# Shared-expert steps of an MoE layer moved between the slot-planning steps of its four token groups

## The chip, the cores and the metric

The kernel runs on one core of a Trainium2 chip. The metric is the device time of one launch in microseconds (us). The core has engines that each take their own instructions strictly in the order in which they were written to that engine's queue: PE (TensorE, matrix products and transposes), DVE (VectorE), ACT (ScalarE, activation functions and copies), POOL (GpSimd, here mostly the issuer of indirect DMAs), and SP (SyncE, which issues the ordinary DMAs). An engine that waits for a semaphore holds up everything behind it in its own queue.

## The reference

The input x has 2 x 1024 tokens of 256 features in fp32. Six residual steps follow one another; `ffn` is a mixture of experts with always-on shared experts, `ln` a layer norm without gain:

```python
x = x + 0.5 * L0_ffn(ln(x))     # 8 experts of width 176, top 2; shared width 352
x = x + L0_attn(ln(x))          # RWKV block: time mix, then channel mix
x = x + 0.5 * L0_ffn(ln(x))     # the same weights again
x = x + 0.5 * L1_ffn(ln(x))     # 32 experts of width 96, top 6; shared width 192
x = x + L1_attn(ln(x))          # linear attention
x = x + 0.5 * L1_ffn(ln(x))

def L0_ffn(x):
    scores = softmax(x @ gate_w); w, i = top_k(scores, 2)
    routed = sum over the chosen experts e of w_e * (silu(x @ w_gate[e]) * (x @ w_up[e])) @ w_down[e]
    shared = silu(x @ sw_gate) * (x @ sw_up) @ sw_down
    return routed + shared

def L0_attn(x):                  # only what the change touches
    h = layer_norm(x); hh = h shifted by one token
    k = (h * tm_mk + hh * (1 - tm_mk)) @ Wk.T   # the same with tm_mv, tm_mr, cm_mk, cm_mr
```

## The kernel before

All of x stays in on-chip memory as 16 tiles of 128 tokens (128 partitions by 256 features). Four tiles make a group, so there are four groups, g = 0 to 3.

One L0 mixture (`sparse_moe` with layer "L0", called once before and once after the RWKV block; the two are called the first and the second mixture here) goes through these steps:

- **prep(g)**: normalizes the group's four tiles, transposes them on PE (L156, tile `pt`), copies the transposes back on ACT (L441, tile `xTs`), multiplies them by the router weights (L453, tile `lg`), and routes: `route` (L174 to L207) takes the softmax and the top 2 on DVE, with the exponential on ACT (L182).
- **plan(g)**: works out a slot for each (token, expert) pair, so that pairs of one expert lie together in blocks of 128. It is a run of small matmuls on PE (L469, L491, L493, L502, L518; tiles `count`, `rank`, `far`) between short DVE operations, and it ends in the index tile `idx` (L557). Group g needs the counts of group g - 1.
- **scatter(g)**: POOL issues eight indirect DMAs (L566), one for each tile and choice, that write the normalized rows to their slots in DRAM (`xs`). After each three of them POOL executes five short `still` memsets (L330, L333).
- **owners()** (L590 to L620): works out which expert owns each block.
- **shared(t0, t1)**: a generator of steps. A step computes the hidden layer of one tile (`shared_hidden`: two gate products `pg` of 352 columns on PE at L659, silu on ACT at L649, a product on DVE at L650), turns that of the tile before (`turn`: three transposes `ph` at L675, copies at L682), and multiplies that of the tile before it by the down weights and adds it to x (`py` at L700, L707). Eight tiles take ten steps.
- **blocks()**: 39 blocks; each is fetched from `xs` by SP (L717, tile `xb`), transposed (L726, tile `px`), multiplied by its expert's weights (L748, then `turn`, then L765) and stored to `ys` (L774). A fetch waits until all 32 scatters have landed. At most five fetches are in flight.
- **combine(g)**: POOL gathers the results back (L785) and DVE adds them to x (L797). It runs beside the blocks.

The tool that records the program does not keep the order in which the Python code issues instructions: it schedules each engine's queue itself, starting from the written order. So instructions can move ahead of others within a stretch, and the order on each engine is fixed when the program is built. Loops that run beside the blocks (`combine`, the RWKV preparation) are placed by a small planner (`Clock`) with estimated block durations, and `behind_blocks()` ties an instruction to the place after the latest block's last instructions.

In the first mixture the written order is: the four groups (`begin`: prep, plan, scatter for each, then owners), `load_rwkv` (which loads the RWKV weights and vectors), the gate weights, the shared experts of the first eight tiles, and then the blocks. Inside `load_rwkv` five small DVE operations (L891) compute 1 - v of the five mixing vectors as each vector's DMA is issued. In the second mixture the order is the same without `load_rwkv`, written out by `slots_of`, and the shared experts stand ahead of the gate weights.

Of the kernel before, what the change touches and what calls it, by code (L numbers as in the profile page):

```python
# [8 lines left out]
F32 = mybir.dt.float32  # L9
I32 = mybir.dt.int32  # L10
AF = mybir.ActivationFunctionType
ALU = mybir.AluOpType
AX = mybir.AxisListType

P = 128
D = 256
DC = D // P
# [5 lines left out]
NB = NTOK // TB  # L23
# [16 lines left out]
def moe_blocks(m, tiles=NT):  # L40
    return (tiles * P * m["K"] + m["E"] * (P - 1)) // P
# [14 lines left out]
def macaron_kernel(ctx: ExitStack, tc: tile.TileContext, a: dict, out: bass.AP):  # L56
    nc = tc.nc
# [59 lines left out]
    def load_square(pool, name):  # L117
        rows, cols = a[name].shape
        w = pool.tile([P, rows // P, cols], F32, name=f"w_{name}")
        nc.sync.dma_start(out=w, in_=a[name].rearrange("(c p) o -> p c o", p=P))  # L120
        return w
# [165 lines left out]
    def fill_slots(xs, n, behind=None):  # L287

        zero = const.tile([P, D], F32, tag="zero", name=f"zero_{n}")
        nc.gpsimd.memset(zero, 0.0)  # L290
        d = nc.sync.dma_start(
            out=xs.rearrange("(n p) d -> p n d", p=P),
            in_=zero.unsqueeze(1).to_broadcast([P, n, D]),
        )
        if behind is not None:
            tc.add_manual_dep(d.ins, behind.name, SYNC, reason="not beside the blocks' loads")
# [10 lines left out]
    class Clock:  # L307
# [46 lines left out]
        def run(self, us):  # L354

            self.end = self.now + us
            while True:
                t = min(self.threads, default=None, key=lambda t: (t[0], t[1]))
                if t is None or t[0] > self.end:
                    break  # L360
                self.now = max(self.now, t[0])
                try:
                    t[0] = next(t[2])
                except StopIteration:
                    self.threads.remove(t)
            self.now = self.end
# [6 lines left out]
        def begin(self, rank, thread):  # L373
            self.threads.append([self.now, rank, thread])
# [13 lines left out]
    @contextmanager  # L388
    def behind_blocks():
        with ExitStack() as st:  # L390
            for d in clock.block.values():
                st.enter_context(tc.issue_after(d))
            yield

    HT = NT // 2
# [485 lines left out]
    rw = {}  # L881

    def load_rwkv(pool):
        for v in ("ln1_g", "ln1_b", "ln2_g", "ln2_b", "tm_first", "tm_mk", "tm_mv", "tm_mr", "cm_mk", "cm_mr"):
            t = pool.tile([P, DC], F32, name=f"v_{v}")
            with nc.allow_non_contiguous_dma(reason="256 numbers, once"):
                nc.sync.dma_start(out=t, in_=a[v].rearrange("(c p) -> p c", p=P))
            rw[v] = t
            if "_m" in v:
                u = pool.tile([P, DC], F32, name=f"u_{v}")  # L890
                nc.vector.tensor_scalar(u, t, -1.0, 1.0, ALU.mult, ALU.add)  # L891
                rw[f"1-{v}"] = u
        for m in ("WkT", "WvT", "WrT", "WoT", "WcrT", "WkeyT", "WvalT"):
            rw[m] = load_square(pool, m)

    def shifted(src, g, bias, tag, b, before, name):


        n = quad(rw["in"], "xn", f"n_{name}", bufs=1)
        normalize(src, n, BT, name)  # L900
        hT = rw["in" if tag == "h1T" else "pool"].tile(
            [P, DC, TB + 1], F32, tag=tag, name=f"hT_{name}", bufs=2
        )
        if before is None:
            nc.vector.memset(hT[:, :, 0:1], 0.0)
        else:
            nc.vector.tensor_copy(hT[:, :, 0:1], before[:, :, TB : TB + 1])
        for c in range(DC):
            nc.scalar.activation(
                hT[:, c, 1 : TB + 1],  # L910
                transposed(n, c, name),
                AF.Identity,
                bias=bias[:, c : c + 1],
                scale=g[:, c : c + 1],
            )
        return hT
# [146 lines left out]
    def wait(done):  # L1063
        while not done():
            yield clock.now + 1.0
# [156 lines left out]

    rwkv = [time_mix_job(0)]

    def slots_of(b):
        def slots():
            m0["prep"](b)
            m0["plan"](b)
            every_step(m0["scatter"](b))

        return slots

    for b in range(1, NB):
        rwkv += [time_mix_job(b), channel_mix_job(b - 1)]
    rwkv.append(channel_mix_job(NB - 1))
# [1 line left out]
    def all_of(part):  # L1237
        for us in part:
            clock.run(us)

    def every_step(part):
        clock.pool = 0.0
        for _ in part:
            clock.pool = 0.0

    def given_rows(m, groups, added, rank=0):

        for g in groups:
            yield from wait(lambda: g in m["ready"])
            yield clock.now + 3.0  # L1250
            yield from m["combine"](g, rank)
            added.add(g)

    def begin(m):

        for g in range(m["groups"]):
            m["prep"](g)
            m["plan"](g)
            every_step(m["scatter"](g))
        m["owners"]()  # L1260

    fill = []

    def settle(*done):

        while not all(d() for d in done):
            if fill:
                all_of(fill.pop(0))
            else:
                clock.run(1.0)  # L1270
# [9 lines left out]
    with ExitStack() as rwkv_stack:  # L1280
        weights = rwkv_stack.enter_context(tc.tile_pool(name="rwkvw", bufs=1))
        rw["in"] = rwkv_stack.enter_context(tc.tile_pool(name="rwkv_in", bufs=1))
        begun = 2
        with tc.tile_pool(name="moe_L0_0", bufs=1) as pool:
            m = sparse_moe("L0", w0, "L0_0", x, xs["L0"], ys["L0"], pool, bufs=1)
            begin(m)
            load_rwkv(weights)
            for h in range(2):
                m["weights"](h)
            every_step(m["shared"](0, HT))  # L1290
            added = set()

            def first_jobs():
                for b in range(begun):
                    yield from wait(lambda: b in added)
                    rwkv[b][0]()

            clock.begin(0, given_rows(m, range(NB), added))
            clock.begin(1, first_jobs())
            all_of(m["blocks"]())  # L1300
            all_of(m["shared"](HT, NT))
            settle(lambda: NB - 1 in added)
        for h in range(2):
            fill_slots(xs["AB"[h]], moe_blocks(MOE["L1"], HT), behind=m["latest"]["add"])
            fill_slots(
                ys["AB"[h]][SURE["L1"] * P :, :],
                moe_blocks(MOE["L1"], HT) - SURE["L1"],
                behind=m["latest"]["add"],
            )
        clock.forget()  # L1310
        rw["pool"] = rwkv_stack.enter_context(tc.tile_pool(name="rwkv", bufs=1))
        early_pool = l0_stack.enter_context(tc.tile_pool(name="early", bufs=1, side="right"))
        m0 = sparse_moe(
            "L0",
            w0,
            "L0_1",
            x,
            xs["L0"],
            ys["L0"],
            early_pool,  # L1320
            bufs=1,
        )
        run(rwkv, begun)
# [4 lines left out]
    load_sparse(w1, "L1", None, 4)  # L1328

    m0["home"]["pool"] = moe_pool  # L1330
    for b in range(NB):
        slots_of(b)()
    m0["owners"]()
    every_step(m0["shared"](0, HT))
    for h in range(2):
        m0["weights"](h)

# [181 lines left out]
```

## Time and profile before

| what | value |
| --- | --- |
| median of 13 runs | 1514.8 us (1507.91 to 1520.51) |
| profiled execution | 1513.09 us, span of its instructions 1511.3 us |
| PE busy | 1277.0 us, 84% of the span |
| DVE, ACT, POOL busy | 740.9, 626.9, 665.5 us |
| the first mixture's groups, to its last scatter | about 8 to 91 us |
| the second mixture's groups, to its last scatter | about 463 to 534 us |

The span is counted from the first profiled instruction; times below are microseconds from there. A busy share is an average over stages that have different limits, so the two stretches in which the groups are planned must be read by themselves: there PE is busy only part of the time. The profile also gives the share of its full clock that TensorE was granted ("PEclk"); at 0.50 every matmul takes about twice as long.

### The profile page before, as it was taken

The page shows a single profiled execution, that of the slowest core. Times are in us where ns is not written, and L with a number is a line of the kernel's source. Part 1 is how long each engine was busy: PE and PEld are TensorE (multiplying, and loading weights), DVE is VectorE, ACT ScalarE, POOL GpSimd, SP SyncE. Part 2 cuts the span into 40 slices and gives each one's busy share as a digit, 9 for nine tenths or more (in the row PEclk, how much of TensorE's full clock was granted, in tenths as well). Part 3 has the DMA queues.
Part 4 walks back from the last instruction along what each step waited for, and adds up shares of the span by engine and source line. Part 5 has one row for each costly group of instructions (what it writes and reads, how often), then busy time and mean ns, then how long its engine had stood idle before and what let it go on. Part 6 is the DMA issues. An engine that isn't in the chain of part 4 may idle for free. (4 is left out here: it accounts for less than half of the span.)

```text
span 1511.3 us, 23078 instructions
## 1 busy us (share of the span) xinstructions
PE 1277.0 (84%) x6100; PEld 978.6 (65%) x6100; DVE 740.9 (49%) x2507; ACT 626.9 (41%) x1672; POOL 665.5 (44%) x1336
## 2 busy tenths in 40 slices
PE   6699889799998799899799789887859888649961
PEld 4677666365576677677588677675647676448941
DVE  5333446845534423564364367655527643416544
ACT  4033544586654133524345354442234443125510
POOL 1630522011102712477774455057765005676565
PEclk9589889799999599999899899988969988769985
DMA  9623424950008324335767575332254323348843
GB/s 284 219 75 109 129 73 157 312 192 1 0 0 191 99 87 130 113 108 149 242 198 242 171 211 157 115 106 98 84 151 149 121 76 129 107 149 265 254 144 94
DMA packets 195170, 214.94 MB, mean 142 GB/s; under 512 B 40892, under 2 KB 178012, under 8 KB 195036
## 3 DMA queue, kind: packets, MB, share of 16 engines
q1 hardware_dynamic: 170460, 146.22, 31.2%
q0 software_dynamic: 24576, 67.14, 14.4%
q8 instruction: 59, 0.97, 0.3%
q14 instruction: 75, 0.61, 0.1%
HBM read 103.04 MB, written 110.23 MB: 141 GB/s over the span
## 5 line engine op out<-in xcount | busy, mean ns | idle before, releaser
L785 POOL DMA_INDIRECT yk_L<-ys_L,idx_L x64 | 62.1, 970 | 187.0 <-DMA ys_L<-yb_L 124.0
L333 POOL MEMSET still<- 128x96 f32 x620 | 111.1, 179 | 35.6
L748 PE MATMUL pg_L_b<-L0gu,xbT_L 128*128 x312 | 110.6, 478 | 0.0
L566 POOL DMA_INDIRECT xs_L<-xn_L,idx_L x64 | 62.0, 969 | 74.6 <-DVE idx_L L557 36.7
L659 PE MATMUL pg_L<-L0sgu,xTs_L 128*128 128x352 f32 x256 | 90.7, 489 | 3.9 <-DVE h_L L650 3.9
L566 POOL DMA_INDIRECT xs_B<-axl_at,idx_L_1B x48 | 46.9, 977 | 100.9 <-DVE idx_L_1B L557 89.2
L785 POOL DMA_INDIRECT yk_L_0B<-ys_B,idx_L_0B x48 | 46.8, 975 | 83.0 <-DMA xb_L_0B<-xs_B 47.3
L765 PE MATMUL py_L_b<-L0down,hT_L_b 88*128 x312 | 81.5, 383 | 0.0
L785 POOL DMA_INDIRECT yk_L_0A<-ys_A,idx_L_0A x48 | 46.6, 971 | 64.4 <-DVE x L797 27.2
L650 DVE TENSOR_TENSOR h_L_b<-g_L_b,pg_L_b 128x176 f32<-128x176 f32 x78 | 26.2, 336 | 95.0 <-ACT g_L_b L649 72.8
L765 PEld LDWEIGHTS py_L_b<-L0down,hT_L_b 88*128 88x128 f32 x312 | 59.4, 194 | 19.7 <-issue 1.5
L748 PEld LDWEIGHTS pg_L_b<-L0gu,xbT_L 128*128 128x128 f32 x312 | 55.8, 197 | 19.4 <-issue 2.0
L934 PE MATMUL pkk_cm<-mk_cm,w_WkeyT 128*128 128x512 f32 x128 | 62.7, 622 | 5.3 <-DVE mk_cm L926 3.6
L659 PEld LDWEIGHTS pg_L<-L0sgu,xTs_L 128*128 128x128 f32 x256 | 48.7, 202 | 27.1 <-DVE h_L L650 5.6
L748 PE MATMUL pg_L_1A_b<-L1gu,xbT_L_1A 128*128 x272 | 63.4, 361 | 0.4 <-PE ph_L_1A_b L675 0.4
L785 POOL DMA_INDIRECT yk_L_1A<-ys_A,idx_L_1A x48 | 46.8, 976 | 29.3 <-DVE h_L_1B_b L650 11.6
L748 PE MATMUL pg_L_0B_b<-L1gu,xbT_L_0B 128*128 x272 | 59.4, 343 | 0.3 <-issue 0.2
L748 PE MATMUL pg_L_0A_b<-L1gu,xbT_L_0A 128*128 x272 | 58.8, 341 | 0.5 <-issue 0.4
L946 PE MATMUL pkv_cm<-w_WvalT,sk_cm 128*128 128x256 f32 x256 | 58.0, 379 | 0.1
L748 PE MATMUL pg_L_1B_b<-L1gu,xbT_L_1B 128*128 x272 | 57.4, 335 | 0.1
L649 ACT ACTIVATE g_L_b<-pg_L_b 128x176 f32<-128x176 f32 x78 | 24.8, 318 | 77.1 <-PE pg_L_b L748 70.5
L566 POOL DMA_INDIRECT xs_A<-xn_L_0A,idx_L_0A x48 | 46.8, 974 | 21.6 <-issue 12.4
(639 smaller groups left out, 3405.7 us busy)
## 6 DMA issues: line engine op xcount, KB each, us to landing
xs_A<-zero SPq DMA_DIRECT2D x1, 10112.0 KB
xs_B<-zero SPq DMA_DIRECT2D x1, 10112.0 KB
xb_L<-xs_L SPq DMA_DIRECT2D x78, 128.0 KB
ys_L<-yb_L SPq DMA_DIRECT2D x78, 128.0 KB
xb_L_0A<-xs_A SPq DMA_DIRECT2D x68, 128.0 KB
ys_A<-yb_L_0A SPq DMA_DIRECT2D x68, 128.0 KB
xb_L_0B<-xs_B SPq DMA_DIRECT2D x68, 128.0 KB
ys_B<-yb_L_0B SPq DMA_DIRECT2D x68, 128.0 KB
```

The source lines that it names most:

```text
L333: d = nc.gpsimd.memset(still, 0.0)
L566: d = nc.gpsimd.indirect_dma_start(out=xs, out_offset=bass.IndirectOffsetOnAxis(ap=idx[:, t, k : k + 1], axis=0), in_=sent[g][t - BT * g], ...
L649: nc.scalar.activation(g, pg[:, 0:width], AF.Silu)
L650: nc.vector.tensor_tensor(dst, g, pg[:, width : 2 * width], ALU.mult)
L659: nc.tensor.matmul(pg, xbT[:, c, i * P : (i + 1) * P], w["sgu"][:, c, u, :, :].rearrange("p z w -> p (z w)"), start=(c == 0), stop=(c == D ...
L748: nc.tensor.matmul(pg, xbT[:, c, :], w["gu"][:, c, bass.ds(e, 1), :, :].rearrange("p e z h -> p (e z h)"), start=(c == 0), stop=(c == DC - 1),
L765: mm = nc.tensor.matmul(py, hT[0:HP, k, :], w["down"][:, bass.ds(e, 1), k, :].rearrange("p e d -> p (e d)"), start=(k == 0), stop=(k == C ...
L785: d = nc.gpsimd.indirect_dma_start(out=yk, out_offset=None, in_=ys[0 : n * P, :], in_offset=bass.IndirectOffsetOnAxis(ap=idx[:, t, k : k + ...
L934: nc.tensor.matmul(ps, w[:, c, oc * P : (oc + 1) * P], src[:, c, :], start=(c == 0), stop=(c == DC - 1),)
L946: nc.tensor.matmul(ps, src[:, c, i * P : (i + 1) * P], w[:, c, :], start=(c == 0), stop=(c == n - 1),)
```

## The change

Three edits. First, `begin` now starts the generator of the first eight tiles' shared experts and takes three of its steps after each group's scatter; what is left (here nothing: 10 steps, taken as 3, 3, 3 and 1) is taken after `owners`. Second, both mixtures use `begin`, so `slots_of` and the separate calls of `shared(0, HT)` go. Third, `load_rwkv` only reserves the five 1 - v tiles; a new function `opposites` computes them, called by the planner's thread `first_jobs` behind the blocks, once group 0 of the first mixture has been added back and just before the first RWKV preparation.

```diff
             rw[v] = t
             if "_m" in v:
-                u = pool.tile([P, DC], F32, name=f"u_{v}")
-                nc.vector.tensor_scalar(u, t, -1.0, 1.0, ALU.mult, ALU.add)
-                rw[f"1-{v}"] = u
+                rw[f"1-{v}"] = pool.tile([P, DC], F32, name=f"u_{v}")
...
+    def opposites():
+
+        for v in [v for v in rw if v.startswith("1-")]:
+            nc.vector.tensor_scalar(rw[v], rw[v[2:]], -1.0, 1.0, ALU.mult, ALU.add)
...
-    def slots_of(b):
-        def slots():
-            m0["prep"](b)
-            m0["plan"](b)
-            every_step(m0["scatter"](b))
-
-        return slots
...
     def begin(m):
 
+        shared = m["shared"](0, HT)
         for g in range(m["groups"]):
             m["prep"](g)
             m["plan"](g)
             every_step(m["scatter"](g))
+            for _ in range(3):
+                next(shared, None)
         m["owners"]()
+        every_step(shared)
...
-            every_step(m["shared"](0, HT))
             added = set()
 
             def first_jobs():
                 for b in range(begun):
                     yield from wait(lambda: b in added)
+                    if b == 0:
+                        with behind_blocks():
+                            opposites()
                     rwkv[b][0]()
...
     m0["home"]["pool"] = moe_pool
-    for b in range(NB):
-        slots_of(b)()
-    m0["owners"]()
-    every_step(m0["shared"](0, HT))
+    begin(m0)
     for h in range(2):
         m0["weights"](h)
```

## The prediction

> **What bounds the kernel now.** I read the page first: the change lies in the two stretches where an L0 mixture plans its groups, so the averages say little there, but two rows do.
>
> ```profile
> PE 1277.0 (84%) x6100; PEld 978.6 (65%) x6100; DVE 740.9 (49%) x2507; ACT 626.9 (41%) x1672; POOL 665.5 (44%) x1336
> ...
> PEclk9589889799999599999899899988969988769985
> ...
> L566 POOL DMA_INDIRECT xs_L<-xn_L,idx_L x64 | 62.0, 969 | 74.6 <-DVE idx_L L557 36.7
> ```
>
> Read in the second row: the clock falls to half in the second of the 40 slices (the first mixture's groups) and again in the fourteenth (the second's). In the third: POOL waits for the indices of the scatters. So next I read the timeline of the second mixture's groups, engine by engine: PE, then DVE, then POOL, then SP and PE again.
>
> ```profile
> 486.49 0.34 PE L469 MATMUL count_L<-ones,taken_L 128*8 128x1 f32 x8 [2.99 <-DVE taken_L L202]
> ...
> 493.72 3.16 PE L453 MATMUL lg_L<-L0router,xTs_L 128*128 128x8 f32 x14 [0.45 <-ACT xTs_L L441]
> ...
> 499.86 0.34 PE L469 MATMUL count_L<-ones,taken_L 128*8 128x1 f32 x8 [2.99 <-DVE taken_L L202]
> ...
> 493.86 0.17 DVE L557 TENSOR_SCALAR idx_L<-top_L 128x8 int32<-128x8 f32 x1
> ...
> 507.24 0.17 DVE L557 TENSOR_SCALAR idx_L<-top_L 128x8 int32<-128x8 f32 x1
> ...
> 521.52 0.17 DVE L557 TENSOR_SCALAR idx_L<-top_L 128x8 int32<-128x8 f32 x1
> ...
> 494.31 0.96 POOL L566 DMA_INDIRECT xs_L<-xn_L,idx_L  x1 [0.46 <-issue]
> ...
> 507.69 0.96 POOL L566 DMA_INDIRECT xs_L<-xn_L,idx_L  x1 [0.53 <-DVE idx_L L557]
> ...
> 521.97 0.97 POOL L566 DMA_INDIRECT xs_L<-xn_L,idx_L  x1 [0.94 <-DVE same_L L629]
> ...
> 535.79 18.25 SPq L717 DMA_DIRECT2D xb_L<-xs_L  x12
> ...
> 543.02 0.38 PE L726 MATMUL px_L<-ident,xb_L 128*128 128x128 f32 x2
> ```
>
> To be seen: the groups' indices come 13.4 and 14.3 us apart, and each group's first scatter starts 0.3 us behind its index, POOL having waited under 1 us. The chain of a group (transposes, logits, routing, plan) is exactly as long as eight scatters: it has no slack. Within it PE idles some 3 us a group, while DVE routes. The fetches are issued at 535.79, but PE takes the first block only at 543.02, because it is still at the shared experts.
>
> The clock, from the windows view:
>
> ```profile
> 478.00:485.00 7.00, 5.16 (x45) 4.52 (x44) 2.35 (x17) 2.90 (x5) 2.81 (x3) 0.97 1.26 256
> 485.00:525.50 40.50, 31.23 (x160) 27.12 (x161) 18.73 (x136) 4.18 (x9) 30.59 (x66) 0.50 0.44 133
> 525.50:545.00 19.50, 19.50 (x93) 15.10 (x93) 5.62 (x16) 7.32 (x25) 6.62 (x15) 1.00 0.25 81
> ```
>
> Half clock through the plans (last but two column) although PE is busy for 31 of 40 us. In windows of one microsecond it is lost between 484 and 485 (0.79), after PE went idle at 483.5, and full again between 525 and 526 (0.73), 3.5 us after the shared gate products begin at 521.88.
>
> In the first mixture the same chain has one wait more, in DVE's timeline:
>
> ```profile
> 51.66 0.20 DVE L891 TENSOR_SCALAR u_tm_mk<-v_tm_mk 128x2 f32<-128x2 f32 x1 [5.13 <-DMA v_tm_mk<-in_tm_mk]
> ...
> 54.04 0.17 DVE L891 TENSOR_SCALAR u_cm_mr<-v_cm_mr 128x2 f32<-128x2 f32 x1 [0.64 <-DMA v_cm_mr<-in_cm_mr]
> 54.12 0.19 DVE L178 TENSOR_REDUCE mx_L<-lg_L 128x4 f32<-128x32 f32 x1
> ...
> 64.90 0.96 POOL L566 DMA_INDIRECT xs_L<-xn_L,idx_L  x1 [6.66 <-DVE idx_L L557]
> ```
>
> Group 2's logits are done at 47.96 (their matmuls run 44.80 to 47.96); its routing stands behind five operations that wait for DMAs, and starts at 54.12.
>
> **The change, part by part.** The built order of the changed program shows where the scheduler puts the shared steps on PE; POOL's and SP's orders stay as they were, but for one swap each far away. Prices, from the second mixture's rows at full and half clock: a gate product `pg` (one of two per tile) 1.18 (526.59 to 527.77) and 2.50 (521.88 to 524.38); a down product `py` 1.30 (528.10 to 529.40) and 2.57 (first mixture, two thirds from 81.59 to 83.30); the three transposes `ph` 0.33 (525.83 to 526.15) and 0.83 (519.68 to 520.51).
>
> *Group 1* (its index is now 13.3 us after group 0's). Ahead of its logits PE gets `ph` of tiles 0 and 1 (0.66), `py` 0 (1.30) and the first halves of the products of tiles 4 and 5 (2.36): +4.3. Their second halves fall into the 3 us in which DVE routes: free. In the plan, `py` 1 and `ph` 2: +1.6. PE comes there busy, so I take full clock: the plan's 5.5 us (486.49 to 492.0) include 1.04 of transposes that move behind, and the other 4.4 become about 2.4 (group 0's plan at full clock, two `far` products fewer, 478.15 to 480.0): -3.0. Sum +2.9.
>
> *Group 2.* Ahead of its logits: four gate products (4.72), `py` 2 and 3 (2.60), `ph` 3 and 4 (0.66): +8.0, at the full clock that such work had at 525.5. Transposes to logits then take about 3.5 instead of 4.95 (491.93 to 496.88): -1.4. Routing leaves PE idle, as now, and the clock was lost there between 484 and 485, so the plan is at half: -1.04 of transposes, + `py` 4 and `ph` 5 (3.4): +2.4. Sum +9.0.
>
> *Group 3.* Ahead of its logits `py` 5 and 6, `ph` 6 and 7: 3.3 at full, 6.8 at half clock; transposes to logits -1.4 or +1.0; `py` 7 in its plan +2.57. Between +4.5 and +10.4; I take 4.5, since the row of 521.88 gave the clock back within 3.5 us of such work.
>
> The sum is +16.4 on the last index, and as the chain has no slack, on the last scatter.
>
> *The other end.* PE is then free when the first block lands. In the later mixture whose first transposes do wait for it, fetch to start is 2.4 us (1340.7 to 1343.1), so blocks can begin at 538.2 and, in the first mixture (fetch 93.00), at 95.4. The first `py` of a block now stands at 552.44 and 110.86: 14.2 and 15.5 after. [...] I take 9.5: -4.7 and -6.0.
>
> *The differences.* Group 2's routing of the first mixture no longer waits: 54.12 - 48.0 = -6.1. The five operations (0.17 to 0.33) now stand on DVE among the adds of group 0, ahead of the RWKV statistics; their DMAs have long landed; DVE is under half busy there: 0, at most +1.1.
>
> *Small ones.* ACT loads tables twice more per mixture (1.28 each, once for group 2's exponential, once for the blocks' silu). The first lies beside 2.2 us of logits, the second beside the first block's product: 0; without cover +5.1 in all. DVE's extra products (0.34) and adds (0.42) end while PE works on: 0, bounds 0 and +3. The RWKV stage is reordered a little (two table loads more): 0, between -3 and +3.
>
> Sum: second mixture 16.4 - 4.7 = +11.7; first 16.4 - 6.1 - 6.0 = +4.3; together +16. Behind the mixtures PE is busy 95 of 100 us (500 to 700), so the delay is carried to the end. Against the profiled 1513.1 us (1.7 below the median of 1514.8) that gives 1529.
>
> [...] The row: from 488 to 491.5 PE never stops and the clock stays at half. [...]
>
> **Rivals.** *The clock stays full* through routing and plans because PE has work between. Then the groups add 2.9, 8.0 - 1.4 + 1.6 - 3.1 = 5.1, and 3.3 - 1.4 + 1.3 - 2.1 = 1.1, together 9.1; blocks gain 7.2 and 8.5: second mixture +1.9, first -5.5. 1509.5, faster by 0.24%. For it: the half clock is dear now. Against it: groups 2 and 3 still have nothing on PE while DVE routes, and 3 us of that cost the clock after 484. It decides once the clock is full in both groups' plans. *The clock stays low*: group 2's burst starts at half (+1.7) and group 3 costs 10.4: 24 per mixture, less 3.9 and 5.2 at the blocks and the 6.1: +33, 1546. For it: light plans never lifted the clock in 40 us. Against: gate products did in 3.5. *No difference*: the shared steps cost the chain only what PE's idle time now holds (9 us a mixture), 16.4 - 9 = 7.4 a mixture, less 4.7, 6.0 and 6.1: -2, 1511 to 1514. Against it: the built order puts only group 1's second halves there.
>
> **How the numbers follow.** Within 0.2% (3 us) a change of this kernel can't be told from none. Chances: the forecast 0.72 (1520 to 1537), low clock 0.13, full clock 0.10, no difference 0.05. The range of 8 in 10 runs from 1514 to 1540; it leaves out most of the full clock and the upper half of the low one. Slower 0.85, same 0.06, faster 0.09.
>
> **What would show it.** Index tiles of the second mixture about 16, 22 and 19 us apart; POOL waiting 3 to 9 us before groups 1 to 3; the last scatter some 15 us later in its stage; PE idle for about 15 us before the first `px`, which starts within 3 us of the first fetch; no L891 wait. Wrong if POOL's waits stay under 1 us, or if the clock is 1.00 through the plans.

## The result and the profile after

The changed kernel takes 1535.7 us (median of 10 executions, 1528.5 to 1540.5) where the kernel before takes 1515.0 (46 executions): a ratio of 1.0128, 95% interval 1.0111 to 1.0145, some 19 us slower. The profiled execution took 1526.9 us (span 1525.1), 13.8 more than the one profiled before. It lies 8.8 us below its own median; that is taken up below.

First the page of the changed kernel, the rows that answer to those shown before:

```profile
PE 1271.6 (83%) x6100; PEld 970.4 (64%) x6100; DVE 738.6 (48%) x2507; ACT 632.6 (41%) x1678; POOL 663.4 (43%) x1336
...
PEclk9859999799999869899899889997879997769985
...
L566 POOL DMA_INDIRECT xs_L<-xn_L,idx_L x64 | 61.8, 966 | 101.3 <-DVE h_L L650 28.7
```

PE is busy for 5 us less, and of the two slices at half clock in the groups (the second and the fourteenth before; the last of the 40 is at half in both kernels) one is left, the third: by averages the kernel got no worse. The third row tells the other side: POOL's idle time ahead of the scatters went from 74.6 to 101.3 us.

The second mixture in DVE's timeline (the four index tiles), then in POOL's (the first scatter of groups 1, 2 and 3), then in SP's and PE's (the first fetch, the first transpose, the first down product of a block). Columns as before: start, duration, engine, line, operation, and in brackets the idle time before it with what ended it.

```profile
484.30 0.17 DVE L557 TENSOR_SCALAR idx_L<-top_L 128x8 int32<-128x8 f32 x1
...
500.45 0.17 DVE L557 TENSOR_SCALAR idx_L<-top_L 128x8 int32<-128x8 f32 x1
...
522.22 0.17 DVE L557 TENSOR_SCALAR idx_L<-top_L 128x8 int32<-128x8 f32 x1
...
540.27 0.17 DVE L557 TENSOR_SCALAR idx_L<-top_L 128x8 int32<-128x8 f32 x1
...
500.90 0.96 POOL L566 DMA_INDIRECT xs_L<-xn_L,idx_L  x1 [3.32 <-DVE same_L L629]
...
522.67 0.96 POOL L566 DMA_INDIRECT xs_L<-xn_L,idx_L  x1 [8.97 <-DVE idx_L L557]
...
540.72 0.96 POOL L566 DMA_INDIRECT xs_L<-xn_L,idx_L  x1 [4.75 <-DVE same_L L629]
...
554.49 12.28 SPq L717 DMA_DIRECT2D xb_L<-xs_L  x12
...
556.62 1.19 PE L726 MATMUL px_L<-ident,xb_L 128*128 128x128 f32 x4 [15.79 <-DMA xb_L<-xs_L]
...
565.18 1.03 PE L765 MATMUL py_L_b<-L0down,hT_L_b 88*128 x4
```

The indices come 16.2, 21.8 and 18.1 us apart (13.4 and 14.3 before). POOL, whose eight scatters last 12 to 13 us, now waits 3.32, 8.97 and 4.75 us before groups 1 to 3. PE then idles 15.8 us for the first block, and needs 10.7 us from fetch to the first down product where it needed 16.7.

The first mixture, in POOL's and DVE's timelines:

```profile
47.22 0.96 POOL L566 DMA_INDIRECT xs_L<-xn_L,idx_L  x1 [4.08 <-DVE same_L L629]
...
69.70 0.96 POOL L566 DMA_INDIRECT xs_L<-xn_L,idx_L  x1 [9.68 <-DVE idx_L L557]
...
90.10 0.96 POOL L566 DMA_INDIRECT xs_L<-xn_L,idx_L  x1 [7.09 <-DVE same_L L629]
...
56.41 0.19 DVE L178 TENSOR_REDUCE mx_L<-lg_L 128x4 f32<-128x32 f32 x1 [4.04 <-PE lg_L L453]
```

The routing of group 2 (last row) no longer stands behind the vectors, but behind its own logits on PE, and starts at 56.41, later than the 54.12 of before.

To compare kernels I use two stage times, read from each profile: from the start of a mixture's first scatter to the start of the first L765 product of its blocks. They leave out most of what the change does not touch.

| kernel | first mixture | second mixture | ratio to before, 95% interval |
| --- | --- | --- | --- |
| before | 78.98 | 70.86 | 1 |
| changed | 85.44 | 79.85 | 1.0128 (1.0111 to 1.0145) |
| e1 differences only | 71.99 | 70.79 | 0.9933 (0.9916 to 0.9950) |
| e2 steps only | 85.40 | 79.94 | 1.0168 (1.0145 to 1.0191) |
| e3 changed, routing filled | 80.08 | 79.72 | 1.0113 (1.0091 to 1.0134) |
| e4 a step in each routing | 70.72 | 67.86 | 0.9993 (0.9972 to 1.0014) |
| e5 second mixture only | 71.94 | 89.22 | 1.0073 (1.0046 to 1.0100) |
| e6 first mixture only | 84.74 | 71.82 | 1.0075 (1.0050 to 1.0100) |
| e7 a step in three routings | 67.81 | 67.25 | 0.9909 (0.9879 to 0.9939) |
| e8 e4's second, first as before | 71.93 | 65.91 | 0.9922 (0.9898 to 0.9946) |
| e9 e1 again | 72.34 | 70.88 | 0.9962 (0.9948 to 0.9975) |
| e10 changed again | 86.42 | 79.82 | 1.0134 (1.0105 to 1.0164) |
| e11 e7's first, e4's second | 68.17 | 69.76 | 0.9925 (0.9908 to 0.9941) |
| e12 changed, plans fed | 79.81 | 77.97 | 1.0119 (1.0095 to 1.0142) |

e1 to e4 ran on one chip, e5 to e8 on a second, e9 to e12 on a third. The kernel before took 1518.2 us on the first and the third and 1495.6 on the second, so only ratios are compared between chips. In the profiles that difference lies behind the second mixture's first block product: 940 to 947 us to the end of the span on the second chip (e5: 1504.2 - 562.90 = 941), 959 to 969 on the others.

The changed kernel's stages took 6.46 and 8.99 us more than before, 15.45 together; the RWKV stretch between them 1.84 less (370.72 to 368.88), the start before the first scatter 0.87 less, the rest behind 1.06 more: 13.80.

### The profile page after: what moved, and what is told of

Same layout as the page of the kernel before. It is cut to its first block, busy times and chain, and to the rows that moved or that the text cites. A ratio compares the mean times of both kernels' runs of the same rounds, so it can differ in the third digit from the quotient of the medians.

```text
span 1525.1 us, 23069 instructions
## 1 busy us (share of the span) xinstructions
PE 1271.6 (83%) x6100; PEld 970.4 (64%) x6100; DVE 738.6 (48%) x2507; ACT 632.6 (41%) x1678; POOL 663.4 (43%) x1336
## 3 DMA queue, kind: packets, MB, share of 16 engines
q0 software_dynamic: 24576, 67.14, 14.3%
## 5 line engine op out<-in xcount | busy, mean ns | idle before, releaser
L748 PE MATMUL pg_L_b<-L0gu,xbT_L 128*128 x312 | 113.7, 490 | 0.4 <-ACT xbT_L L730 0.4
L566 POOL DMA_INDIRECT xs_L<-xn_L,idx_L x64 | 61.8, 966 | 101.3 <-DVE h_L L650 28.7
L659 PE MATMUL pg_L<-L0sgu,xTs_L 128*128 128x352 f32 x256 | 87.1, 471 | 3.7 <-DVE h_L L650 3.7
L765 PE MATMUL py_L_b<-L0down,hT_L_b 88*128 x312 | 81.9, 385 | 0.0
L765 PEld LDWEIGHTS py_L_b<-L0down,hT_L_b 88*128 88x128 f32 x312 | 59.5, 194 | 19.9 <-issue 1.2
L726 PE MATMUL px_L<-ident,xb_L 128*128 128x128 f32 x156 | 31.3, 287 | 39.7 <-DMA xb_L<-xs_L 31.4
```

The source lines that it names most:

```text
L566: d = nc.gpsimd.indirect_dma_start(out=xs, out_offset=bass.IndirectOffsetOnAxis(ap=idx[:, t, k : k + 1], axis=0), in_=sent[g][t - BT * g], ...
L659: nc.tensor.matmul(pg, xbT[:, c, i * P : (i + 1) * P], w["sgu"][:, c, u, :, :].rearrange("p z w -> p (z w)"), start=(c == 0), stop=(c == D ...
L726: nc.tensor.transpose(px[:, c * P : (c + 1) * P], xb[:, c * P : (c + 1) * P], ident)
L748: nc.tensor.matmul(pg, xbT[:, c, :], w["gu"][:, c, bass.ds(e, 1), :, :].rearrange("p e z h -> p (e z h)"), start=(c == 0), stop=(c == DC - 1),
L765: mm = nc.tensor.matmul(py, hT[0:HP, k, :], w["down"][:, bass.ds(e, 1), k, :].rearrange("p e d -> p (e d)"), start=(k == 0), stop=(k == C ...
```

## Experiments: the parts one by one

**e1: the differences alone.** The kernel before with one part of the change:

```diff
-                u = pool.tile([P, DC], F32, name=f"u_{v}")
-                nc.vector.tensor_scalar(u, t, -1.0, 1.0, ALU.mult, ALU.add)
-                rw[f"1-{v}"] = u
+                rw[f"1-{v}"] = pool.tile([P, DC], F32, name=f"u_{v}")
...
+                    if b == 0:
+                        with behind_blocks():
+                            opposites()
                     rwkv[b][0]()
```

> The kernel before with one edit of the change: the five 1 - v operations are computed by opposites() behind the blocks; the shared steps stay where they were. Theory A (the prediction's term of -6.1): group 2's routing in the first mixture no longer waits for the vectors, POOL's wait of 6.66 us ahead of group 2's first scatter goes (under 1 us is left), everything behind it is 6 us earlier: 1509 us, -0.4%. Rival B (the wait is passed on): another late DMA or DVE's order holds group 2 as long; 1515 us, and POOL still waits over 4 us there.

1507.9 us, ratio 0.9933. e1's DVE and POOL in the first mixture's group 2:

```profile
47.51 0.19 DVE L178 TENSOR_REDUCE mx_L<-lg_L 128x4 f32<-128x32 f32 x1 [1.46 <-PE lg_L L453]
...
58.30 0.96 POOL L566 DMA_INDIRECT xs_L<-xn_L,idx_L  x1 [0.55 <-issue]
```

The routing starts with its logits, POOL's wait of 6.66 is 0.55, the stage is 7.0 us shorter. Theory A: this part of the change is a gain. How large is less sure than one run says: e9, the same kernel on a third chip, was expected at 0.9933 within 0.002 and with executions within 4 us, and came out at 0.9962 with executions 7 us apart. By these two runs the gain is 0.4 to 0.7%, and the ratios of one kernel from two chips lie 0.3% apart.

**e2: the shared steps alone**, the same hunks undone in the changed kernel.

```diff
-                rw[f"1-{v}"] = pool.tile([P, DC], F32, name=f"u_{v}")
+                u = pool.tile([P, DC], F32, name=f"u_{v}")
+                nc.vector.tensor_scalar(u, t, -1.0, 1.0, ALU.mult, ALU.add)
+                rw[f"1-{v}"] = u
...
-                    if b == 0:
-                        with behind_blocks():
-                            opposites()
```

> The changed kernel with the differences put back into load_rwkv; the shared steps stand between the groups in both mixtures. Theory A, as the prediction added it up: the wait for the vectors (6.1 us) comes back on top of the shared steps: 1542 us, 6 above the changed kernel's 1535.7. Rival B: the two do not add. The shared steps alone make group 2's logits of the first mixture late (56.3 us in the changed kernel's profile, against 54.0 when the last of the five was done before), so the wait lies beside PE's work: 1536 us, equal to the changed kernel within 2 us, and the five operations are done before group 2's routing could start.

1541.4 us, theory A's number. But the wait is in another place than theory A had it. e2's DVE, in the slot computation of group 1:

```profile
47.31 0.19 DVE L546 SCALAR_TENSOR_TENSOR slot_L<-rank_L,slot_L 128x32 f32<-128x32 f32 x1
...
50.34 0.17 DVE L891 TENSOR_SCALAR u_tm_mk<-v_tm_mk 128x2 f32<-128x2 f32 x1 [2.84 <-DMA v_tm_mk<-in_tm_mk]
...
52.42 0.17 DVE L891 TENSOR_SCALAR u_cm_mr<-v_cm_mr 128x2 f32<-128x2 f32 x1 [0.61 <-DMA v_cm_mr<-in_cm_mr]
...
53.13 0.17 DVE L557 TENSOR_SCALAR idx_L<-top_L 128x8 int32<-128x8 f32 x1
```

In the order that was built here the five operations stand in the middle of group 1's slots and hold its index until 53.13 (46.78 in the changed kernel): POOL waits 10.08 us before group 1 instead of 4.08. In the profile groups 2 and 3 make most of that good again (7.50 and 4.75 instead of 9.68 and 7.09), and the stage is 85.40 for the changed kernel's 85.44: there the two delays do not add, as theory B said, though not by its account, since it is a different group that waits. The medians are 0.4% apart (the intervals just touch), but the profiles put that elsewhere: of the 8 us by which e2's span is longer, 5.8 lie behind the second mixture's first block product (965.7 and 959.9). That theory A's number came out is therefore not shown to be the wait for the vectors.

**e5 and e6: one mixture each**, the differences moved in both. The diff of e5 (e6 has 3 and 0 exchanged):

```diff
-    def begin(m):
+    def begin(m, n):
...
-            for _ in range(3):
+            for _ in range(n):
                 next(shared, None)
...
-            begin(m)
+            begin(m, 0)
...
-    begin(m0)
+    begin(m0, 3)
```

> The changed kernel with the first mixture written as before (its eight shared tiles behind the groups); the second mixture and the differences as changed. Theory A (each mixture pays for its own groups, the differences pay back once): the differences alone took 1507.9 us; first scatter to first product of a block takes 79.9 us in the second mixture of the changed kernel's profile and 70.8 where only the differences moved: +9.1, 1517 us. Theory B (the 9 us by which the changed kernel's median lies above its profiled execution come from the second mixture): 1526 us, with executions more than 8 us apart.

> The reverse: the shared steps between the groups of the first mixture alone, the second mixture as before, the differences moved. Theory A: first scatter to first product of a block 85.4 us in the changed kernel's profile, 72.0 with only the differences moved: +13.4, 1521 us; together with the run of the second mixture alone the two delays add up to the changed kernel's. Theory B (the changed kernel's spread between executions, 12 us, comes from the first mixture, whose steps stand beside loads that fill the DMA engines): 1526 to 1530 us, with executions more than 8 us apart, and those of the second mixture alone within 4.

1.0073 and 1.0075. Against e1's 0.9933 each mixture costs 1.4% (1.1% against e9's 0.9962), more than the 0.6 and 0.9% that theory A took from the profile; the two add up to 2.8% (2.2%), and the changed kernel lies 2.0% above e1 on other chips, 1.7% on one chip (e10's median 1538.3 and e9's 1512.1). On the spread, e5's executions lie 15 us apart, as its theory B asked, and e6's 7, where its theory B asked for over 8 and for e5's within 4: neither mixture is shown to be the only source. e5's own profile shows why its second mixture is dearer than the changed kernel's, with the same instructions in the same order. First POOL, then the windows view of e5 (window; length; busy time and count of PE, PEld, DVE, ACT, POOL; granted clock; DMA share; GB/s):

```profile
492.84 0.95 POOL L566 DMA_INDIRECT xs_L<-xn_L,idx_L  x1 [6.91 <-DVE same_L L629]
...
518.27 0.96 POOL L566 DMA_INDIRECT xs_L<-xn_L,idx_L  x1 [12.61 <-DVE idx_L L557]
...
538.59 0.97 POOL L566 DMA_INDIRECT xs_L<-xn_L,idx_L  x1 [7.00 <-DVE same_L L629]
...
482.00:485.00 3.00, 2.48 (x20) 1.60 (x18) 2.59 (x23) 2.14 (x5) 1.93 (x8) 1.00 1.15 305
485.00:488.00 3.00, 3.00 (x15) 2.58 (x15) 0.27 (x2) 0.00 (x0) 0.94 (x1) 0.72 0.37 127
488.00:491.00 3.00, 3.00 (x12) 2.38 (x11) 1.41 (x7) 0.53 (x2) 0.00 (x0) 0.50 0.00 0
...
497.00:500.00 3.00, 3.00 (x15) 2.22 (x14) 1.03 (x4) 0.85 (x3) 2.30 (x8) 1.00 0.25 90
```

and the same stretch, group 1's plan, of the changed kernel:

```profile
493.00:496.00 3.00, 2.48 (x24) 1.88 (x22) 2.01 (x17) 1.15 (x5) 2.24 (x7) 1.00 1.16 309
496.00:499.00 3.00, 3.00 (x17) 2.48 (x18) 1.33 (x6) 0.53 (x2) 1.27 (x2) 1.00 0.83 220
499.00:502.00 3.00, 3.00 (x15) 2.28 (x14) 2.57 (x19) 0.85 (x3) 1.10 (x2) 1.00 0.00 0
```

In the one execution group 1's plan runs at full clock, in the other the clock falls to half in it and stays there for some ten microseconds of plan and shared work, with PE busy for 3.00 of 3.00. The groups wait 26.5 us instead of 17.0. The last section has the two executions side by side.

## Experiments: the clock

**e3: PE fed through the routing.** Unused gate products between logits and plan of groups 2 and 3 of the changed kernel:

```diff
+        def again(t):
+
+            _, xbT, i = places(t)
+            W = SH // SU
+            pz = bank("py", f"pz_{name}_{t}")[:, 0 : 2 * W]
+            for z in range(4):
+                nc.tensor.matmul(
+                    pz,
+                    xbT[:, 1, i * P : (i + 1) * P],
+                    w["sgu"][:, 1, z % 2, :, :].rearrange("p z w -> p (z w)"),
+                    start=(z == 0),
+                    stop=(z == 3),
+                )
...
             m["prep"](g)
+            if g > 1:
+                m["again"](BT * g)
             m["plan"](g)
```

> The changed kernel, and PE gets four gate products more (352 columns each, their result is not used) between the logits and the plan of groups 2 and 3, in both mixtures, so that it is not idle for the 3 us of the routing. The computation is otherwise the changed kernel's. Theory A (the groups' cost is partly the half clock that the idle routing brings): PEclk 1.00 in the plans of groups 2 and 3; by the changed kernel's rows that takes about 3 and 6.5 us off group 2's plan (second and first mixture) and 4.5 off each of group 3's: 18 us in all, 1517 us (1512 to 1524). Rival B (the delay is the number of products ahead of the logits, and the clock's fall lies beside waits for DVE and POOL): no change within 4 us, 1532 to 1540, whatever the clock does.

1534.7 us, 1.0113: theory B's number, and a miss of 18 us for A. The products stand where they should (507.0 to 509.6 in the second mixture, the plan's first matmul 0.57 us behind them), but the clock does not stay. e3's windows over group 2's plan:

```profile
510.00:512.00 2.00, 1.80 (x21) 1.76 (x21) 1.09 (x7) 0.00 (x0) 0.81 (x1) 1.00 0.22 74
512.00:514.00 2.00, 2.00 (x10) 1.65 (x9) 0.20 (x1) 0.00 (x0) 0.00 (x0) 0.81 0.02 4
514.00:516.00 2.00, 2.00 (x9) 1.65 (x8) 0.99 (x4) 0.53 (x2) 0.00 (x0) 0.50 0.00 0
```

It falls at 513.2, inside the plan (0.81 over 2 us), with PE busy for 2.00 of 2.00; in the changed kernel it fell at 512.5, 2.5 us into 3.04 us of idle time. So here it fell without the idle time of the routing. The first mixture took 5.4 us less in this one profile, the second no less.

**e12: the plans fed as well**, two more such products inside each group's plan:

```diff
+            if name[0:2] == "L0":
+                again(lo, 2)
             pb = bank("pt", f"far_{sub}")
...
+            if g > 1:
+                m["again"](BT * g, 4)
```

> The changed kernel with unused gate products that keep PE at wide work: four of 352 columns between logits and plan of groups 2 and 3 as in the run that filled the routing, and two more inside every group's plan, ahead of far. They add 1.2 us of PE to each group's chain (some 10 us in all with group 0's). Theory A (in the plans the clock falls although PE is busy, because products of 1 to 32 columns do not keep it up; that is where the spread and half of the groups' cost come from): PEclk 1.00 through all plans, executions within 6 us of each other, ratio 1.000 to 1.007, so faster than the changed kernel in spite of more work. Theory B (the clock is not what delays the groups): the added work shows, ratio 1.013 to 1.025, spread 12 us as before.

1.0119, executions 1530 to 1541. e12's windows over the plans of groups 1, 2 and 3 of the second mixture:

```profile
494.00:497.00 3.00, 2.48 (x22) 1.84 (x21) 1.90 (x16) 1.00 (x5) 2.24 (x7) 1.00 1.10 293
...
515.00:518.00 3.00, 3.00 (x20) 2.21 (x16) 0.75 (x5) 0.00 (x0) 0.10 (x1) 1.00 0.13 46
...
530.00:533.00 3.00, 2.58 (x22) 2.36 (x23) 1.29 (x8) 0.00 (x0) 2.42 (x5) 0.92 0.27 93
533.00:536.00 3.00, 3.00 (x17) 1.75 (x16) 0.00 (x0) 0.00 (x0) 1.88 (x7) 0.50 0.24 87
```

With wide products in it, the clock stays full through the plans of groups 1 and 2 and falls only in group 3's (0.92 of the third window). The stages are 6.6 and 1.9 us shorter than in e10 on the same chip, although 1.2 us of PE were added to the chain of each of groups 1 to 3: by that the half clock costs an estimated 10 us in the first mixture and 5.5 in the second (6.6 and 1.9, plus 3.6 each; one profile of each kernel). But the feeding takes much of that away again: the median moves by 5 us against e10's (1538.3 to 1533.3), and the executions stay 10 us apart. Theory A was right on the clock row but for group 3, and too high on what it is worth; as the spread stays with the plans fed, the clock in the plans is not shown to be its main source.

**e10: the changed kernel once more.**

> The changed kernel, unedited, for a second profile of it and for the sum on one chip. Theory A (the spread of 12 us between its executions is the clock: the same instructions in the same order, and whether it falls in the plans of groups 1, 2 and 3 differs from execution to execution): ratio 1.013 again; first scatter to first product of a block lies between 80 and 89 us in the second mixture and PEclk differs there from the first profile where the time does. Theory B (the spread has nothing to do with the clock): stage times differ by several us at the same PEclk row.

Ratio 1.0134. The profiled execution took 1536.5 us, 9.6 more than the first one, with almost the same stages (86.42 and 79.82). It lost its time later: 968.7 us from the second mixture's first block product to the end (1534.7 - 566.03), against 959.9 (1525.1 - 565.18) and 958.9 before. That stretch holds no line of the change. Compared instruction by instruction, e10 is 0.9 us behind the first profile up to 735 us and 9.6 at 1419 us, so it lost its time in the L1 stages. So A is wrong for these two executions: the clock did differ (in the first mixture: 0.7 in the second slice of e10's page for 0.8, and POOL waited 5.72 us before group 1 for 4.08), but that stage is only 1 us longer. The kernel before has a spread of 14 us too; whether it arises in the same place, and what varies in the L1 stages, is open.

## Experiments: shared work inside the wait for the routing

**e4: one step inside the routing** of each group in place of three behind each scatter.

```diff
             m["prep"](g)
+            next(shared, None)
             m["plan"](g)
             every_step(m["scatter"](g))
-            for _ in range(3):
-                next(shared, None)
```

> The changed kernel with one shared step between each group's logits and its plan, where PE waits for the routing, in place of three steps after each scatter; what is left follows owners() as it does there. Theory A (only PE work ahead of the logits and the half clock cost time): a step's gate products (2.4 us) fit the 3 us of routing, the plans run at full clock, POOL waits under 1.5 us before every group, some 10 us of shared work are left for the 14 us of the last scatters and the first fetch; blocks start about 5 us earlier in each mixture and the wait for the vectors is gone: 1499 us (1495 to 1508). Rival B (what costs is that the shared steps' operations on DVE and ACT, with two table loads of 1.28 us a group, stand among the routing's): the groups stay 2 to 4 us late each, 1515 to 1530 us.

The stages are 70.7 and 67.9, shorter than with the differences alone, and POOL's waits 1.35 and 4.59, 1.66 and 1.61 (none before group 2): A's picture, in the profile. Yet the median is 1518.0 and the executions run from 1505 to 1523; the profiled one is the fastest of the twelve, and why the others show none of the gain is open. The gain over e1 in the stages, 1.3 and 2.9 us, is less than hoped: PE runs out of shared work 5.3 us before the first block lands, and the clock is at half for that block (0.50 from 92 to 98 in the first mixture; in the second its first two gate products take 2.71 and 2.44 us, the next 1.35): 12.3 and 12.0 us from fetch to first down product.

**e7, e8, e11: fewer steps.** `begin` takes a step only in the groups named; what is left follows, in the first mixture behind `load_rwkv` and the gate weights, as in the kernel before.

```diff
+            if g in within:
+                next(shared, None)
...
-            begin(m)
+            shared = begin(m, (0, 1, 2))
...
+            every_step(shared)
...
-    begin(m0)
+    every_step(begin(m0, (0, 1, 2)))
```

(e8: no group in the first mixture and all four in the second; e11: (0, 1, 2) and (0, 1, 2, 3).)

> One shared step between logits and plan of groups 0, 1 and 2, in both mixtures; the steps left, some 17 us of PE at full clock, follow owners(). Group 3 keeps its plan free. Theory A (a step in the routing costs a group 0 to 1.7 us, in group 3 1.6 to 4.6, and shared work that lasts until the first block lands keeps the clock full for the blocks): no wait over 2 us on POOL, PE busy up to the first block, first product of a block 9 us behind the first fetch and not 12; 1501 us in the profile. Theory B (the gain of four steps over none, 2.4 us in the profile, is all there is, and with it comes a spread of 18 us between executions): 1508 to 1518 us, no better than the differences alone.

> One shared step between logits and plan of all four groups in the second mixture alone; the first mixture as before, the differences moved. Theory A: first scatter to first product 67.9 us in the profile with four steps in both, 70.8 with none: -2.9, 1505 us. Theory B (the spread of the run with four steps in both, 1505 to 1523 us, has its cause in the first mixture): all executions within 4 us here, as with the differences alone; if the cause lies in the second mixture, they are again more than 10 us apart.

> One shared step between logits and plan of groups 0, 1, 2 in the first mixture and of all four in the second; the differences moved. Theory A (the best stage times of the two runs before add up: 67.8 us from first scatter to first product of a block in the first mixture, 65.9 in the second, against 72.0 and 70.8 with the differences alone): 9 us less than the differences alone, ratio 0.987 to 0.990. Theory B (what shared work in the routing gains in a profile is lost again in the other executions by the clock): 0.993 or more, executions 8 us or more apart.

0.9909, 0.9922 and 0.9925. With the three steps, PE has shared work until the block lands, as theory A of e7 had it: the first down product comes 10.2 and 10.3 us behind the first fetch (88.88 to 99.06 and 526.14 to 536.40; 9 were expected), the waits are 2.76 and 2.42, 2.98 and 1.47, a little over its bound of 2. e8's executions lie 7 us apart, not within the 4 that its theory A asked, but no further than those of the differences alone (e9), so e4's spread does not come from the second mixture alone. e11 beats e9, the differences alone, by 0.4% on the same chip (0.9925 against 0.9962, the intervals apart), less than the 9 us expected: its second mixture took 69.8 us with two waits of 3 us, where the same code took 65.9 in e8. It is faster than both the kernel before and the changed one; e7 and e8 have ratios no worse, but ran on another chip.

## Why the prediction was right

Its forecast, 1529 us by way of +16 in the two mixtures, stood against a measured +15.5 in the mixtures, +13.8 in the profile and +19 by the ratio. The mechanism held, link by link, as the items below show. That the sum of the mixtures is so close has some luck in it: +11.7 and +4.3 were forecast for the second and the first, +8.99 and +6.46 were measured, and the two misses cancel.

- *The groups.* The waits of 3.32, 8.97 and 4.75 in the second mixture are, less the 0.46, 0.53 and 0.94 of before, +2.9, +8.4 and +3.8 for the forecast +2.9, +9.0 and +4.5, and the indices come 16, 22 and 18 us apart for 16, 22 and 19. From its first scatter to its last that mixture takes 15.0 us more (66.6 and 51.7), not 16.4.
- *The other end.* Gains of 6.0 and 5.3 us for 4.7 and 6.0; the first block finds PE idle for 15.8 us, as forecast, and the clock at half (0.50 from 556.62 to 560.30). The 9.5 us that the sum takes from a block's first transpose to its first down product, and the rivals' gains there (7.2 and 8.5, 3.9 and 5.2), were the author's estimate, which no run shows; the runs showed 8.6 us in the second mixture (556.62 to 565.18), the first 3.7 of them at half clock, and 10.6 in the first (105.83 to 116.45), the first 7.4 at half.
- *The differences.* -7.0 in e1 (-6.6 in e9) for -6.1. The wait itself went from 6.66 to 0.55, which is the 6.1; most of the rest lies between the first fetch and the first down product (17.9 to 16.4 in e1). That it does so only where group 2 is the group that waits was missing: e2 shows the same operations holding group 1.
- *Mis-sized: group 3 of the first mixture.* "I take 4.5" of 4.5 to 10.4; the wait measured 7.09 (0.94 before), because the clock came back only at 72.2, 9.8 us after the first down product in group 2's plan (62.44), and not within 3.5 us of shared work. Groups 1 and 2 came out as forecast (4.08 for 1.37 before, 9.68 for 6.66); with the smaller gain at the other end the first mixture cost 6.5 us for the 4.3 in the sum.
- *Wrong in its reason: "Routing leaves PE idle ... so the plan is at half".* Half it was (0.50 from 512.6 to 519.3), but e3 took the idle time away and the clock fell all the same, at 513.2, with PE busy for 2.00 of 2.00 us. With wide products put among the plan's small ones as well it stayed at 1.00 through that plan (e12, 512 to 521). Nor do the rows of the kernel before give one reason: there the clock fell at 484.59, after 1.1 us of idle time, and from 488 to 491.5, with PE busy for 3.50 of 3.50 us, it stayed at 0.50. What decides is not shown; the last section has what the runs put beside it.
- *The rival "the clock stays low"*, 24 us a mixture, had 0.13; e5's second mixture comes near it in sum, with 26.5 us of waits (24.6 more than before), but not in its terms: group 1, where the rival expected no more than the forecast, waits 6.91, and group 3 7.00 for 10.4. The order of instructions in that mixture is that of the forecast's case; the execution is another.
- *Small ones.* ACT's table for the exponential (508.29 to 509.57) lies beside the logits (508.32 to 510.05), as taken. The RWKV stretch came out at -1.8, taken as 0.
- *Not foreseen:* that the kernels lie 6 us further apart by the ratio than in the profiles. e10 and e5 show two places where executions of the same instructions differ, the L1 stages and the groups with their clock; how the 6 us divide is open.

## What to carry to other kernels

Where a chain across engines is as long as the transfers it feeds, work moved between its links costs most of its length, even on an engine that is idle for a quarter of the time (9.3 of 40.5 us here): look up in the built order what it stands ahead of, not how much idle time there is. The place that costs little is inside the chain's own wait for another engine (e7, e8 and e11; e4 in its profile alone), and the amount is the one that lasts until the next stage's data lands. A wait for a small DMA in a queue that others depend on (five operations of 0.2 us here) is worth moving by itself, and may be worth more alone than the change that it came with, as here.

## What the runs showed of the hardware

The clock can fall to half while PE is busy: in e5 at 486.3 (0.72 over 485 to 488), 2.2 us after the first small matmul of a plan (1 to 32 columns), with 0.53 us of idle time ahead of them, and it stays there for ten microseconds of back-to-back work, wide products among it. With two products of 352 columns (1.2 us) put among the small ones it stays full (e12, groups 1 and 2: 1.00 over 494 to 500 and 512 to 521). The same instructions in the same order on PE met this in group 1 in one execution and not in another: 89.2 and 79.9 us for one stage. Half clock takes wide products twice as long (the four matmuls of one gate product `pg` 2.71 and 1.35 us), but not every matmul: a plan's eight `count` products of one column take 0.34 us at either clock.

The two executions lie side by side as follows. In e5 the `count` products of group 1's plan start at 484.13 and the clock falls at 486.3. In the changed kernel they start at 494.14, with 0.52 us of idle time ahead of them, and the clock is 1.00 from 493 to 502. From there to the first block it is at half in the changed kernel from 512.5 to 519.4 and from 529.6 to 560.3; in e5 from 486.3 to 496.6, from 506.8 to 520.5 and from 527.3 to beyond 548. Why the one lost the clock in group 1 and the other did not is not shown.

PE's busy time does not tell what the clock does. These are e8's second mixture and e11's first, two stretches of each, in the windows view:

```profile
489.35:492.75 3.40, 2.04 (x17) 1.16 (x15) 2.44 (x21) 2.36 (x5) 2.73 (x4) 1.00 0.23 80
492.76:496.16 3.40, 3.40 (x24) 2.99 (x23) 0.94 (x4) 0.10 (x1) 2.64 (x6) 1.00 0.21 77
...
52.27:55.66 3.39, 3.39 (x32) 2.94 (x31) 0.67 (x4) 0.90 (x2) 2.69 (x7) 1.00 0.97 299
55.68:59.08 3.40, 2.95 (x14) 2.86 (x15) 1.83 (x14) 1.87 (x2) 2.70 (x8) 0.50 0.96 304
```

In e8 PE is idle for 1.36 of the first 3.40 us, and the clock is 1.00 in both rows; in e11 it is never idle in the first row (3.39 of 3.39), and the second is at 0.50. This is read from the runs as they are. Only e12 put wide work into the plans on purpose, and there the clock fell in group 3's plan (0.92 over 530 to 533, then 0.50): that a wider plan would keep the clock in every group is not shown.
